# The head of each image woven into the layers of the next one, with its state and residual sum kept in HBM

## Chip, cores and metric

The kernel runs on one core of one Trainium2 chip. The metric is the device time of one launch in microseconds, which covers all eight images of the batch. A launch is repeated and the median is given.

## The reference

The input `x` has shape (8, 8, 256, 256): eight images of eight channels. Layer 0 of the network is a Fourier neural operator on the group-normalised image, added to its input. Layer 1 is a 3x3 dilation of the group-normalised result, again added to its input.

```python
h = _gconv1x1(concat(xg, grid), fc0_w, fc0_b)        # 4 groups, 10 channels each
for i in range(4):
    h1 = _spectral_conv(h, sp_w1[i], sp_w2[i])       # 24 x 12 modes mixed, rest zero
    h2 = _gconv1x1(h, w_w[i], w_b[i])
    h = h1 + h2
    if i < 3:
        h = _gswish(h, betas[i])
h = _gswish(_gconv1x1(h, fc1_w, fc1_b), betas[3])    # 10 -> 128 channels per group
return _gconv1x1(h, fc2_w, fc2_b)                    # 128 -> 2 per group
...
x = x + _L0_conv_ref(_gn(x), ...)
x = x + _L1_conv_ref(_gn(x))                         # max over 3x3 windows, border -2
```

## The kernel before

Images are handled one after another. The state of one image, 40 channels of 256 x 256, lives in SBUF as `h`, 11 chunks of 128 partitions by 4 x 512 numbers. Each of the four layers has the same stages.

- The spectrum of the state is formed. For layer 0 `spectrum_x` takes it from the image by transposes (L204), a Fourier product (L214) and small products (L223, L233). For the later layers each chunk is turned on VectorE as soon as it is written (`turn`, L394) and multiplied with the Fourier table (`transform`, L407: 128 small products of 32 x 32 for a pair of chunks, 256 records in the profile), and `spectrum_h` does the other direction (L268 or L285, then L293).
- `mix` multiplies the modes by the weights, all on VectorE (L322, L326, six of each), and folds them (L338) into `fz`.
- `rows_of` transforms back along one axis (L358 or L363) into the tile `Z`.
- `layer` writes one chunk at a time: 16 products for the pointwise weights (L439 for layer 0, L442 later) and 8 for the other axis (L445) go to two PSUM tiles `p_z`. The document calls these a burst. ScalarE applies Silu from PSUM into `h` (L450). In layer 3 VectorE and ScalarE add a bias instead (L452, L454).

After layer 3, `head` runs 128 steps. In a step, `first` makes 512 hidden values of 128 partitions for each of four groups (L482, two PSUM tiles), ScalarE applies two Silus of 128 x 1024 (L485), and `second` of the step before adds its products (L491) to a sum `acc` that lasts 16 steps. Then `residual` (L496) adds the image on VectorE into the tile `x1`. After step 80 the head is interrupted by `prologue`: the spectrum and the first mix of the next image. After the head, `dilate` takes statistics of `x1`, fetches the neighbour rows by DMA (L522, L523) and works in four pieces (L529 to L542), each sent out by SP (L543).

PSUM is one pool of four tiles of two banks, from which every product takes its tiles:

```python
ps = ctx.enter_context(tc.tile_pool(name="ps", bufs=4, space=PSUM))
def ps_z(name):
    return ps.tile([128, 2, 512], F32, tag="z", name=name)
def ps_a(name):
    return ps_z(name)[:, 0, :]
```

Each engine works through its own queue in order. TensorE's order is the order of the program text within the blocks marked `manual_schedule`. On the other engines a scheduler of the framework chooses the order from its own estimate of when operands are ready. All DMAs are issued by SP.

Of the kernel before, what the change touches and what calls it, by code (L numbers as in the profile page):

```python
# [1 line left out]

# [15 lines left out]
C = 8  # L18
# [18 lines left out]
PIX = 2 * HW  # L37


@with_exitstack  # L40
def fno_dilate_kernel(ctx: ExitStack, tc: tile.TileContext, a: dict, out: bass.AP):
# [6 lines left out]
    ps = ctx.enter_context(tc.tile_pool(name="ps", bufs=4, space=PSUM))  # L48

    def ps_z(name):  # L50
        return ps.tile([128, 2, 512], F32, tag="z", name=name)

    def ps_a(name):
        return ps_z(name)[:, 0, :]
# [10 lines left out]
    def load_x(b):  # L65
        t = sb.tile([128, 4096], F32, tag="x", bufs=1, name=f"x_{b}")
        nc.sync.dma_start(t, a["x"][b].rearrange("c (p f) -> (c p) f", p=16))
        return t

    x_tiles = {0: load_x(0)}  # L70
# [12 lines left out]
    eh_f = load("eh_f", (NQ * CS, 3, NBLK, 32))  # L83
# [16 lines left out]
    for c in range(NCH):  # L100
        nc.gpsimd.memset(h[:, c], 0.0)
    fz = const.tile([128, WID, G, 32], F32, tag="fz", name="fz")
# [66 lines left out]
    def group_stats(chunks, name):  # L169
        n = len(chunks)  # L170
        st = sb.tile([128, n, 6], F32, tag="bn", name=f"bn_{name}")
        for i, c in enumerate(chunks):
            nc.vector.bn_stats(st[:, i, :], c)
        mv = sb.tile([128, 2], F32, tag="mv", name=f"mv_{name}")
# [3 lines left out]
        mr = sb.tile([128, 2], F32, tag="mr", name=f"mr_{name}")  # L178
# [12 lines left out]
    def spectrum_x(b):  # L191

        x = x_tiles[b]
        mr = group_stats([x[:, 512 * i : 512 * (i + 1)] for i in range(8)], f"x{b}")
        a0 = sb.tile([128, 128, 16], F32, tag="A", bufs=1, name=f"a0_{b}")
        for half in range(2):
            xn = x[:, 2048 * half : 2048 * (half + 1)]
            nc.vector.tensor_scalar(xn, xn, mr[:, 0:1], mr[:, 1:2], ALU.subtract, ALU.mult)
            xn = xn.rearrange("p (r w) -> p r w", r=8)
            xt = sb.tile([128, 2, 8, 128], F32, tag="ht", name=f"xt_{b}_{half}")  # L200
            for r in range(0, 8, 2):
                t = ps_a(f"p_xt_{b}_{half}_{r}")
                for i in range(4):
                    nc.tensor.transpose(  # L204
                        t[:, 128 * i : 128 * (i + 1)],
                        xn[:, r + i // 2, 128 * (i % 2) : 128 * (i % 2 + 1)], ident,
                    )
                nc.vector.tensor_copy(
                    xt[:, :, r : r + 2, :], t.rearrange("p (r f c) -> p f r c", r=2, f=2)
                )  # L210
            for i in range(2):
                p = ps_a(f"p_a0_{b}_{half}_{i}")
                for f in range(2):
                    mm(p[:32, :], fw[:, f, :], xt[:, f, 4 * i : 4 * i + 4, :],  # L214
                       start=f == 0, stop=f == 1)
                r0 = 8 * half + 4 * i
                nc.vector.tensor_copy(
                    a0[:32, :, r0 : r0 + 4], p[:32, :].rearrange("p (r c) -> p c r", r=4)
                )
        x2 = sb.tile([128, C, 2, 32], F32, tag="xs", name=f"x2_{b}")  # L220
# [6 lines left out]
        nc.vector.tensor_copy(x2.rearrange("p c f k -> p (c f k)"), t)  # L227
        p = ps_a(f"p_xs_{b}")
# [14 lines left out]
        prod = sb.tile([128, 6, G, WID, 5], F32, tag="ht", name=f"prod_{b}")  # L243
# [8 lines left out]
        return bt, mr  # L252
# [5 lines left out]
    def spectrum_h(b, l, at):  # L258

        rows = sb.tile([128, NBLK * WID * 128], F32, tag="big", bufs=1, name=f"AT_{b}_{l}")  # L260
        if l % 2 == 1:

            view = rows.rearrange("p (i g k) -> p i g k", g=G, k=32)
            for j0 in range(0, NBLK * WID, 8):
                n = min(8, NBLK * WID - j0)
                t = ps_z(f"p_at_{b}_{l}_{j0}")
                for i in range(n):
                    nc.tensor.transpose(  # L268
                        t[: NQ * CS, i // 4, 128 * (i % 4) : 128 * (i % 4 + 1)],
                        at[:, :, :, j0 + i], ident)  # L270
                dst = rows[: NQ * CS, 128 * j0 : 128 * (j0 + n)]
                src = t[: NQ * CS].rearrange("p u w -> p (u w)")[:, : 128 * n]
# [4 lines left out]
            eh, m = eh_f, NQ * CS  # L277
            read = lambda blk, k0: view[:m, WID * blk : WID * (blk + 1), :, k0 : k0 + 3]
        else:

            view = rows.rearrange("p (g i k) -> p i g k", g=G, k=32)
            for i in range(4):
                cut = at[:, NBLK * WID * i : NBLK * WID * (i + 1), :]
                over = bass.AP(cut.tensor, cut.offset, [cut.ap[0], cut.ap[1], [1, 32]])
                nc.vector.transpose(rows[:, 960 * i : 960 * (i + 1)].rearrange("p (i r) -> p i r", r=32), over)  # L285
            eh, m = eh_q, 128
            read = lambda blk, k0: view[:m, WID * blk : WID * (blk + 1), :, k0 : k0 + 3]
        p = ps_a(f"p_b_{b}_{l}")
        for k in range(2):
            for n in range(2 * NBLK):  # L290
                term, blk = n // NBLK, n % NBLK
                for q in range(4):
                    mm(p[part(q), 120 * k : 120 * k + 120], eh[:, spectrum_table(k, term), blk, :],  # L293
                       read(blk, 12 * term + 3 * q), start=n == 0, stop=n == 2 * NBLK - 1)
# [10 lines left out]
        return bt  # L305

    def load_sw(b, l):
        tiles = []
        for k in range(3):
            t = sb.tile([128, G, 2 * WID, WID], F32, tag="xs", name=f"sw_{b}_{l}_{k}")  # L310
            nc.sync.dma_start(t.rearrange("p g m i -> p (g m i)"), a["spw"][l, k])
            tiles.append(t)
        return tiles

    def mix(b, l, bt):

        s = [sb.tile([128, 3, G, 2, WID], F32, tag=f"S{i}", bufs=1, name=f"S{i}_{b}_{l}") for i in range(2)]
        sw = load_sw(b, l)
        for k in range(3):
            for k2 in range(2):  # L320
                pr = sb.tile([128, G, 2 * WID, WID], F32, tag="ht", name=f"pr_{b}_{l}_{k}_{k2}")
                nc.vector.tensor_tensor(  # L322
                    pr, sw[k], bt[:, k2, k].unsqueeze(2).to_broadcast([128, G, 2 * WID, WID]),
                    ALU.mult,
                )
# [6 lines left out]
        nc.vector.tensor_tensor(f[:, 1], s[0][:, :, :, 1, :], s[1][:, :, :, 0, :], ALU.add)  # L332

# [7 lines left out]
        for q in range(4):  # L341
# [4 lines left out]
            else:  # L346
                nc.scalar.copy(dst, src)  # L347

    def rows_of(b, l):

        z = sb.tile([128, CS, NQ, 32], F32, tag="big", bufs=1, name=f"Z_{b}_{l}")
        nc.gpsimd.memset(z[:, :, :, NBLK * WID :], 0.0)
        zv = z[:, :, :, : NBLK * WID].rearrange("p r f (n o) -> p o n r f", n=NBLK)
        for o in range(0, WID, 2):
# [10 lines left out]
            for u in range(2):  # L365
                src = p[:, u, : NBLK * CS * NQ]
                if l % 2 == 0:
                    dst, src = zv[:, o + u].rearrange("p n r f -> p n f r"), src.rearrange("p (n f r) -> p n f r", n=NBLK, r=CS)
# [7 lines left out]
        return z  # L376


    def layer(b, l, z, mr=None):
        at = None  # L380
        if l == 1:

            at = sb.tile([128, G * NBLK * WID + 1, 24], F32, tag="A", bufs=1, name=f"A_{b}_{l}")
            nc.gpsimd.memset(at[:, :, CS:], 0.0)
            nc.gpsimd.memset(at[:, G * NBLK * WID], 0.0)
        elif l < 3:
            at = sb.tile([128, NQ, CS, 32], F32, tag="A", bufs=1, name=f"A_{b}_{l}")
        ht = {}

        def turn(c):  # L390

            if c % 2 == 0:
                ht[0] = sb.tile([128, 2, NQ, 2, 8, 32], F32, tag="ht", name=f"ht_{b}_{l}_{c}")
            nc.vector.transpose(  # L394
                ht[0][:, c % 2].rearrange("p f s v i -> p (f s v i)"),
                h[:, c].rearrange("p f w -> p (f w)"),
            )
            return (ht[0], c // 2, 2) if c % 2 == 1 else ((ht[0], c // 2, 1) if c == NCH - 1 else None)

        def transform(t, d, n):  # L400

            m = 2 * n * NBLK * WID
            pair = [ps_z(f"p_d_{b}_{l}_{d}_{i}") for i in range(2)]
            for v in range(8):
                for f in range(NQ):
                    for q in range(NQ):
                        mm(pair[q // 2][part(f), q % 2, :m], fw8[part(q), v, :],  # L407
                           t[part(q), :n, f, :, v, : NBLK * WID], start=v == 0, stop=v == 7)
            for i in range(2):
                src = pair[i][:, :, :m]  # L410
                if l == 1:
                    dst = at[:, : G * NBLK * WID].rearrange("p (q i) r -> p q i r", q=NQ)[
                        :, 2 * i : 2 * i + 2, :, 4 * d : 4 * d + 2 * n]
                    src = src.rearrange("p q (r i) -> p q i r", i=NBLK * WID)
                else:
                    dst = at[:, 2 * i : 2 * i + 2, 4 * d : 4 * d + 2 * n, : NBLK * WID]
                    src = src.rearrange("p q (r i) -> p q r i", i=NBLK * WID)
                if i == 0:
                    nc.vector.tensor_copy(dst, src)
                else:  # L420
                    nc.scalar.copy(dst, src)  # L421
# [8 lines left out]
        ready = []  # L430
        with tc.manual_schedule(engines={PE}):
            for c in range(NCH):
                pair = [ps_z(f"p_z_{b}_{l}_{c}_{i}") for i in range(2)]
                for f in range(NQ):
                    for q in range(NQ):
                        o = pair[q // 2][part(f), q % 2, :]
                        if l == 0:
# [279 lines left out]
```

## Time and profile before

| | us |
|---|---|
| runs shown: median (lowest to highest of 3) | 5554.56 (5548.94 to 5554.61) |
| the profiled execution | 5550.97 |
| its span, first to last instruction | 5549.1 |
| PE busy in the span | 4317.3 (78%) |
| PE weight loads, beside PE | 1945.8 (35%) |
| DVE busy | 2002.1 (36%) |
| ACT busy | 2848.7 (51%) |
| POOL busy | 38.5 (1%) |
| mean granted TensorE clock | 0.872 |
| HBM read, written | 91.87 MB, 16.78 MB |

Busy times of the engines overlap, so they don't add up to the span. PE is TensorE, DVE is VectorE, ACT is ScalarE, POOL is GpSimd and SP is the engine that issues DMAs. The granted clock is the share of full speed at which TensorE was let run. In lines of the profile, `L482` is a line of the kernel, `out<-in` are tiles, `xN` is the number of instructions, and a bracket at the end of a line of the timeline says how long the engine was idle and what ended it.

### The profile page before, as it was taken

How to read it: one execution, taken by the hardware profiler on the slowest of the kernel's cores; microseconds unless marked ns; L12 is line 12 of the kernel's file. 1: busy time of each engine (PE TensorE's matmuls, PEld its weight loads, DVE VectorE, ACT ScalarE, POOL GpSimd, SP SyncE). 2: the span in 40 equal slices, each digit the busy share in tenths (PEclk: the TensorE clock that was granted, in tenths of full speed). 3: DMA queues.
4: the chain of work that ended last, by engine and by line, in shares of the span. 5: the costliest groups of instructions: out<-in, count | busy, mean ns of one | idle time of the engine just before them, and what ended most of it. 6: DMA issues, size and time to landing. Idle time of an engine off the chain costs nothing.

```text
span 5549.1 us, 169821 instructions
## 1 busy us (share of the span) xinstructions
PE 4317.3 (78%) x80490; PEld 1945.8 (35%) x80490; DVE 2002.1 (36%) x2363; ACT 2848.7 (51%) x3117; POOL 38.5 (1%) x99
## 2 busy tenths in 40 slices
PE   5679876798667986679866798667986679866897
PEld 3442234422344223442234422344223442234421
DVE  6440344403454035530355303453035530355302
ACT  2248642486324863248632486334863248623486
POOL 1000000000000000000000000000000000000000
PEclk8889877999789997899868898689997899978998
DMA  2000000000000000000100000000000000000000
GB/s 75 21 21 9 30 27 21 21 10 29 27 21 22 9 29 27 21 22 9 30 26 21 22 9 29 27 21 22 9 31 26 21 22 12 13 29 18 22 1 17
DMA packets 46814, 121.60 MB, mean 22 GB/s; under 512 B 6783, under 2 KB 26471, under 8 KB 42983
## 3 DMA queue, kind: packets, MB, share of 16 engines
q1 hardware_dynamic: 46119, 110.75, 6.6%
q8 instruction: 630, 10.32, 0.8%
q14 instruction: 65, 0.53, 0.0%
HBM read 91.87 MB, written 16.78 MB: 20 GB/s over the span
## 4 chain that ended last, share of the span: by engine, by line
PE 73%; DVE 16%; issue 8%; ACT 2%; DMA 0%; DVEq 0%; SPq 0%; ACTq 0%
PE p_fc L482 22%; PE p_fc L491 18%; PE p_d L407 10%; PE p_z L445 7%; PE p_z L442 5%; DVE pr L322 3%; PE p_z L439 2%; DVE S L326 2%; PE p_g L363 2%; PE p_b L293 2%; PE p_at L268 1%; PE p_g L358 1%; PE p_f L338 1%; DVE h L429 1%; DVE m L529 1%
## 5 line engine op out<-in xcount | busy, mean ns | idle before, releaser
L485 ACT ACTIVATE act<-p_fc 128x1024 f32<-128x1024 f32 x2048 | 1982.5, 1021 | 249.0 <-PE p_fc L482 233.0
L482 PE MATMUL p_fc<-h,c_w 32*128 32x512 f32 x8192 | 1298.2, 642 | 7.8 <-DVE h L452 4.1
L491 PE MATMUL p_fc<-act,c_w 128*32 128x512 f32 x8192 | 1104.9, 605 | 0.3
L394 DVE STREAM_TRANSPOSE ht<-h 128x2048 f32<-128x2048 f32 x264 | 599.7, 2297 | 601.0 <-ACT h L450 600.3
L407 PE MATMUL p_d<-ht,c_fw 32*32 32x120 f32 (+1 forms) x36864 | 565.0, 283 | 276.3 <-issue 274.1
L482 PEld LDWEIGHTS p_fc<-h,c_w 32*128 32x128 f32 x8192 | 439.6, 184 | 864.8 <-issue 545.9
L450 ACT ACTIVATE h<-p_z 128x1024 f32<-128x1024 f32 x528 | 511.9, 1021 | 382.4 <-PE p_z L445 382.3
L407 PEld LDWEIGHTS p_d<-ht,c_fw 32*32 32x32 f32 x36864 | 467.3, 109 | 391.6 <-issue 346.2
L496 DVE SCALAR_TENSOR_TENSOR x<-p_fc,c_b,x 128x512 f32<-128x512 f32 x64 | 48.1, 752 | 1501.2 <-PE p_fc L491 1215.3
L445 PE MATMUL p_z<-c_binv,Z 32*128 32x256 f32 x5632 | 463.1, 443 | 14.1 <-ACT Z L375 9.0
L347 ACT COPY fz<-p_f 32x240 f32<-32x240 f32 x64 | 35.5, 554 | 819.7 <-DVE fz L345 819.7
L491 PEld LDWEIGHTS p_fc<-act,c_w 128*32 128x32 f32 x8192 | 163.7, 108 | 792.9 <-issue 726.7
L445 PEld LDWEIGHTS p_z<-c_binv,Z 32*128 32x128 f32 x5632 | 287.4, 205 | 363.7 <-issue 350.1
L338 PE MATMUL p_f<-F,c_fold 32*32 32x120 f32 x1024 | 58.3, 402 | 442.1 <-DVE F L331 442.1
L442 PE MATMUL p_z<-h,c_wt 32*32 32x512 f32 x8448 | 352.6, 610 | 20.8 <-issue 20.7
L421 ACT COPY A<-p_d 128x240 f32<-128x240 f32 x144 | 49.8, 346 | 598.8 <-PE p_d L407 598.8
L375 ACT COPY Z<-p_g 128x264 f32<-128x264 f32 x160 | 96.4, 629 | 385.9 <-DVE Z L373 360.5
L358 PE MATMUL p_g<-c_rowg,fz 128*128 128x264 f32 x320 | 116.2, 536 | 226.8 <-ACT Z L375 203.3
L429 DVE TENSOR_SCALAR h<-h,mr_x 128x2048 f32<-128x2048 f32 x88 | 117.4, 1334 | 382.0 <-DMA h<-in_xp 381.5
L338 PEld LDWEIGHTS p_f<-F,c_fold 32*32 32x32 f32 x1024 | 44.9, 163 | 450.7 <-issue 352.1
L322 DVE TENSOR_TENSOR pr<-sw,B 128x800 f32<-128x800 f32 x192 | 182.2, 980 | 0.6
L326 DVE TENSOR_REDUCE S<-pr 128x80 f32<-128x800 f32 x192 | 181.2, 975 | 0.8
(131 smaller groups left out, 2287.5 us busy)
## 6 DMA issues: line engine op xcount, KB each, us to landing
sw<-in_spw SPq DMA_DIRECT2D x96, 400.0 KB
x<-in_x SPq DMA_DIRECT2D x16, 2048.0 KB
h<-in_xp SPq DMA_DIRECT2D x352, 48.0 KB
out<-o SPq DMA_DIRECT2D x32, 512.0 KB
x<-x SPq DMA_DIRECT2D x16, 112.0 KB
c_wt<-in_wt SPq DMA_DIRECT2D x1, 256.0 KB
x<-x SPq DMA_DIRECT2D x16, 15.0 KB
c_w<-in_w SPq DMA_DIRECT2D x1, 192.0 KB
```

The lines of the kernel that those rows point to most:

```text
L322: nc.vector.tensor_tensor(pr, sw[k], bt[:, k2, k].unsqueeze(2).to_broadcast([128, G, 2 * WID, WID]), ALU.mult,)
L326: nc.vector.tensor_reduce(s[k2][:, k].rearrange("p g s o -> p (g s o)"), pr.rearrange("p g m i -> p (g m) i"), AX.X, ALU.add,)
L358: mm(p[:, u, : NBLK * CS * NQ], fz[:, o + u].rearrange("p g k -> p (g k)"), rowg.rearrange("p n j r -> p (n j r)"), start=True, stop=True)
L394: nc.vector.transpose(ht[0][:, c % 2].rearrange("p f s v i -> p (f s v i)"), h[:, c].rearrange("p f w -> p (f w)"),)
L407: mm(pair[q // 2][part(f), q % 2, :m], fw8[part(q), v, :], t[part(q), :n, f, :, v, : NBLK * WID], start=v == 0, stop=v == 7)
L429: nc.vector.tensor_scalar(hc, hc, mr[:, 0:1], mr[:, 1:2], ALU.subtract, ALU.mult)
L442: mm(o, wt[part(q), l, g, :], h[part(q), c, f, :], start=True, stop=False)
L445: mm(pair[q // 2][:, q % 2, HW * s : HW * (s + 1)], z[part(q), 2 * c + s].rearrange("p f o -> p (f o)"), binv[part(q), :], start=False, st ...
L450: nc.scalar.activation(dst, pair[i], AF.Silu)
L482: mm(pair[g // 2][:, g % 2, :], w1[gs, blk, :], h[gs, c, j, :], start=True, stop=True)
L485: nc.scalar.activation(act[:, 2 * i : 2 * i + 2, :], pair[i], AF.Silu)
L491: mm(acc[32 * g : 32 * g + 32, :], w2[:, g, 15 - rb : 47 - rb], act[:, g, :], start=rb == 0, stop=rb == 15)
```

## The change

The head of image b no longer follows its layers. After layer 3 each chunk of the state is stored to HBM (`stored`), and the next image's layers start at once. `layers` is now a generator that gives way after each small part and says how many units the part counts. The main loop runs head steps of the image before so that 128 of them spread evenly over one image's units. `unit` emits a burst and then the second half of whatever came before it, which was held back in `late`. The head reads the state back from HBM, a chunk at a time. The residual sum goes to HBM too (`y_rows`), and the dilation, now in eight pieces of two output rows (`DR = 2`), reads four rows per piece into the single tile `yin`. A dilation advances by one of its three parts with each head step of the following image. Image 0's layers and the last head and dilation have no partner.

PSUM becomes three tiles of two banks (`z`) and two tiles of one bank (`a`). The tiles for images, turned chunks and products share one constant tile `turned`. The transform's result goes back into `Z`. The loads of the head and all DMAs of the dilation are issued by POOL; the stores of the state are issued by SP.

```diff
-    ps = ctx.enter_context(tc.tile_pool(name="ps", bufs=4, space=PSUM))
+    ps = ctx.enter_context(tc.tile_pool(name="ps", bufs=2, space=PSUM))
+    dram = ctx.enter_context(tc.tile_pool(name="dram", bufs=2, space=bass.MemoryType.DRAM))
     def ps_z(name):
-        return ps.tile([128, 2, 512], F32, tag="z", name=name)
+        return ps.tile([128, 2, 512], F32, tag="z", bufs=3, name=name)
     def ps_a(name):
-        return ps_z(name)[:, 0, :]
+        return ps.tile([128, 512], F32, tag="a", bufs=2, name=name)
...
+    turned = const.tile([128, 3, 2048], F32, tag="turned", name="turned")
+    yin = const.tile([128, DR + 2, HW + 2], F32, tag="yin", name="yin")
...
+    def unit(burst, after):
+        burst()
+        if late[0] is not None:
+            late[0]()
+        late[0] = after
...
     # layer()
+        for c in range(NCH):
+            before = ready[c - 1] if l < 3 and c > 0 else None
+            unit(partial(burst, c), partial(transform, before) if before is not None else None)
+            yield 1
+        if l < 3:
+            yield 2
+            if before not in done:
+                flush()
+            transform(ready[NCH - 1])
+            yield 1
     # burst(c), at its end
+            if l < 3:
+                ready.append(turn(c))
+            else:
+                nc.sync.dma_start(stored[c], h[:, c].rearrange("p f w -> p (f w)"))
...
+    def load_state(b, c, stored):
+        t = sb.tile([128, NQ, PIX], F32, tag="hs", name=f"hs_{b}_{c}")
+        nc.gpsimd.dma_start(t.rearrange("p f w -> p (f w)"), stored[c])
     # head(), second(n) at the end of 16 steps
+                y = box["y"]
+                nc.vector.scalar_tensor_tensor(y, acc, b2, y, ALU.add, ALU.add)
+                nc.vector.bn_stats(stats[:, t, :], y)
+                whole = y_rows[b % 2][:]
+                nc.gpsimd.dma_start(
+                    bass.AP(whole.tensor, whole.offset + (1 + 2 * t) * HW, [[16 * HW, 128], [1, 512]]), y)
+        for n in range(STEPS):
+            if n % 12 == 0 and n // 12 + 1 < NCH:
+                hs[n // 12 + 1] = load_state(b, n // 12 + 1, stored)
+            unit(partial(first, n), partial(second, n))
+            yield
...
     # dilate()
+        for r in range(0, 16, DR):
+            nc.gpsimd.dma_start(
+                yin[:, :, 1 : HW + 1],
+                bass.AP(whole.tensor, whole.offset + r * HW, [[16 * HW, 128], [HW, DR + 2], [1, HW]]))
+            yield
...
+            nc.vector.tensor_tensor(m, yin[:, :, 0:HW], yin[:, :, 1 : HW + 1], ALU.max)
...
+            yield
...
+            nc.vector.tensor_tensor(o, o, yin[:, 1 : DR + 1, 1 : HW + 1], ALU.add)
+            nc.gpsimd.dma_start(o_rows[:, HW * r : HW * (r + DR)], o.rearrange("p r w -> p (r w)"))
+            yield
...
+    with tc.manual_schedule(engines={PE}):
+        for b in range(n_img):
...
+            for n in layers(b, stored):
+                count += n
+                if total is not None:
+                    share += n * STEPS / total
+                    while share >= 1.0:
+                        share -= 1.0
+                        step()
```

The function `step` advances the oldest head by one step and, beside it, the oldest dilation by one part.

## The prediction

> **What bounds the kernel now.** I read the slices of the span first, then groups, waits and, for one image, the timeline.
>
> ```profile
> PE   5679876798667986679866798667986679866897
> DVE  6440344403454035530355303453035530355302
> ACT  2248642486324863248632486334863248623486
> PEclk8889877999789997899868898689997899978998
> ```
>
> Eight images, eight waves: ACT climbs to 8 where a head runs and falls to 2 where layers run; DVE does the opposite. PE is full in heads only. Nothing is full throughout, so the time is a sum of stages, each with its own limit. Stretches of one image (core time, PE busy, PEld, DVE, ACT, POOL, granted clock, DMA):
>
> ```profile
> 740.00:760.00 20.00, 0.00 (x0) 0.00 (x0) 20.00 (x27) 0.00 (x0) 0.00 (x0) 0.50 0.13 52
> 980.00:1020.00 40.00, 31.70 (x1399) 20.73 (x1385) 19.03 (x12) 15.28 (x19) 0.00 (x0) 1.00 0.02 4
> 1100.00:1120.00 20.00, 20.00 (x152) 5.38 (x144) 0.00 (x0) 17.89 (x19) 0.00 (x0) 1.00 0.05 11
> ```
>
> The first is the dilation: PE idle, clock at half. The second is inside a layer, the third the head: PE full, ACT at 89%. The timeline of a layer's two-chunk cycle:
>
> ```profile
> 1008.02 1.15 PE L445 MATMUL p_z<-c_binv,Z 32*128 32x256 f32 x16
> 1009.09 1.18 PE L442 MATMUL p_z<-h,c_wt 32*32 32x512 f32 x32
> 1009.20 1.94 ACT L450 ACTIVATE h<-p_z 128x1024 f32<-128x1024 f32 x2 [3.86 <-PE p_z L445]
> 1010.21 1.15 PE L445 MATMUL p_z<-c_binv,Z 32*128 32x256 f32 x16
> 1011.28 2.56 PE L407 MATMUL p_d<-ht,c_fw 32*32 32x120 f32 x180
> 1015.86 1.17 PE L407 MATMUL p_d<-ht,c_fw 32*32 32x120 f32 x72 [2.02 <-issue]
> ```
>
> A burst (L442 then L445) takes 2.18 us, its two Silus on ACT 1.94; a transform (L407, 256 records at about 14 ns) takes 3.6 us plus a hole in which nothing was issued. Two waits matter (total us, times, longest):
>
> ```profile
> PE p_f L338 <- DVE F L331: 442.1, 32, 20.3
> PE p_d L407 <- issue: 274.1, 183, 2.5
> ```
>
> The first is the mix on DVE: 11.3 us (848.6 to 859.9) with PE empty. The second is the hole.
>
> Image 1, 724 to 1418 us, splits so: dilation and first rows to the first burst 43 us; layers 0, 1, 2 from first burst to the following table work 72.5, 67.5, 61 (sum 201); the three pieces between layers 32, 31, 33.5 (sum 96.5); layer 3 24; the head 175 + 111 = 286, for 128 steps of 2.18 (L482 1.15, L491 1.0); the prologue inside it 43. Sum 694.
>
> **What the Trainium skill says.** "TensorE: Matmul & The Clock Gate", Part 1 (HAM clock gate): after an idle window of about 3.4 us the array clock halves. The trace agrees: 0.50 at 740 to 760. "Runtime: NRT & Kernel Launch", Instruction fetch mechanics: instructions come in blocks of 256. The trace fits two blocks of lead: the holes come after 130 to 240 transform records, each of these being a load and a multiply. The page gives PE room for 2048, which the trace does not support. "DMA: Bandwidth & Descriptors", Anatomy of one DMA (SWDGE): a POOL-issued DMA costs 2.0 us + bytes/436e3; no run shows one yet. "TensorE: Matmul & The Clock Gate", Engine queue depths: ACT and DVE are strict FIFO; so I use the instruction order of the built program.
>
> **The change part by part, per woven image.**
>
> *Removed:* the x1 tile with its four halo copies on SP (L522, L523), the prologue inside the head, the dilation with PE idle. *Added:* 11 stores and 11 loads of the state, 8 stores of y, 8 loads of yin of four rows each, 8 `out` stores of 256 KB for 4 of 512 KB. *Moved:* the head's steps into the next image's layers, the dilation into the one after, one piece in three steps.
>
> *Floor.* At full clock PE work is 128 steps 279, 44 bursts 96, 18 transforms 63 (15 pairs of 3.6, three singles of 2.9), p_g 22 and transposes, tables and spectrum 36, both scaled from their rows: 496 us. What comes on top is waiting, and it is the question here.
>
> *Layers 0 to 2.* PE order per two chunks: burst, second, first, transform, burst, second, first. PSUM falls from four z buffers to three, taken in turn. A step adds two Silus in ACT's FIFO behind the burst's two. From a burst's end, ACT needs 0.17 + 3 x 1.0 to free the third buffer, PE has second and first (2.15) to do: the transform's second buffer is 1.3 us late, and the next burst without a transform between 1.15 late. The burst after a transform waits for its copies (two of 0.28 and the way there): 0.85. The hole stays, about 1.7, as a transform still is 512 instructions in a row. Cycle: 4.36 + 4.36 + 3.6 + 1.7 + 1.3 + 1.15 + 0.85 = 17.3. Five cycles 86.5, one burst 2.2, 1.6 extra steps 3.4, tail (3.4 steps 7.5, last transform 4.6) 12: 104 us with 16 steps inside. Less 34.9 for those: 69, against 67 before. Three layers: lose 6. The two-chunk cycle before, about 10.6, plus two steps is 15: here weaving gives nothing.
>
> *Layer 3.* Same third-buffer wait: 5.15 per chunk and an extra step in seven, 60 us with 12.6 steps; net 32.5 against 24: lose 8.5.
>
> *Between layers.* The mix's 11.3 + 1.3 us on DVE are covered by 7 steps (15.2). p_at 4.4, p_b 3.4, 13.7 steps 29.9, p_f with the four alternating fz copies 3.7, p_g about 4: 45 us; for layer 2, where DVE turns the table, 42; for layer 3 again 45, sum 132. p_g's copies stand on ACT behind a step's two Silus, which I count as covered by the next step; net 132 - 89.6 = 42.5 against 96.5: gain 54.
>
> *Image start (spectrum, mix, rows, dilation of an earlier image).* DVE order matters here: six of eight dilation pieces lie among the spectrum's copies, and a piece's first max stands right behind the last add of the piece before, on one yin buffer. DVE work: eight pieces of 5.46 (two max of 1024 at 1.22 as in L532; of 512, estimated from the same rows, three at 0.75 and a scaling 0.45; two edges 0.32) 44, eleven L429-like scalings at 1.33 15, mix 12, statistics, copies and products 20: 91. Waits for yin: each load is out store, then load on POOL's queue, behind DVE's add: 1.0 (my estimate of the issue) + 2.0 + 524288/436e3 = 4.3, fully exposed in about four pieces, 17 in all; the first (y store, then load) 8. Sum 116; behind it p_g and six steps 18: 134 us. PE's own work there is about 80, so it stands about 50: 8 at p_sv, whose operand is queued on DVE behind the first yin load, 8 in the first half of the spectrum and 12 in the second, 8 at p_xs and p_f, 14 at p_g, whose fz copies stand behind the last piece. Steps cannot fill this, since PE's queue is in order and the waiting instruction stands ahead of them. Net of 26 steps (56.7) 77, against 43 + 43 before: gain 9. Cost of a load, both ends: 2.7 (small SP copies that DVE awaited at L525, issue to use) to 10.
>
> *State through HBM.* 88 stores of 1 MB on SP in layer 3, 88 loads on POOL two ahead: a load's estimate 4.4 us against 26 us for 12 steps even undisturbed. Hidden; I take 0, at worst 2 us per load where it slows PE's instruction blocks: 20 per image. It cannot gain. The xp loads on SP now stand between these stores, but their scalings are due only in the next image start: 0, or up to 10 if a store lags. On POOL an hs load waits for its buffer with y loads, y stores and Z's memsets queued behind; by the instruction order none of these is due before that buffer falls free, so 0; in the worst case a memset delays p_g by one step interval, about 5. The Sqrt of the two statistics still switches ACT's table (1.28 each way): same number, 0.
>
> Woven image: 134 + 3 x 104 + 60 + 132 = 638, against 694.
>
> *Ends.* Image 0, not woven: heads started at 398; three buffers cost 2.1 per cycle (16.5 of them) and 1.2 per chunk in layer 3, constants are now loaded ahead of x (8): 454. Last head 279. Last dilation alone: 8 + 8 x (4.3 + 5.5) = 86 and 2 for the store, against 38.
>
> Sum: 454 + 7 x 638 + 279 + 88 = 5287, +2 outside the span: 5290. The profiled execution took 5551 (span 5549.1) and the median is 5554.6, so they compare directly: -4.7%.
>
> **Rivals.** (a) PE packs nearly full: the waits overlap the holes, or DVE drains faster, so an image falls to 500 to 580 us; 454 + 7 x 540 + 367 = 4600, at best 4300. For it: the floor of 497. Against: two Silus of burst and step share one FIFO. (b) Slower: DVE stands for yin at each image start. If a load takes 10 us instead of 4.3, seven pieces cost 40 us more per image, 280 in all: 5570; from about 9.6 us per load on it decides (262 us of gain over seven images and seven pieces is 5.3). For it: one yin buffer, write and read through HBM, POOL issuing in order behind waits. Against: 512 KB is small and the rings are nearly idle (2 to 5%). (c) The added waits in layers return the whole gain (2.3 us more per cycle than I count, times 16.5 is 38 per image, 266): 5556, no change. For it: sixteen holes and PSUM waits per image whose overlap I only reckoned by hand.
>
> **How the numbers follow.** Mild gain (5000 to 5530) 0.64; (a) below 5000 0.10; within 0.2%, about what a measurement of this kernel can tell from no change, 0.04 (mostly from c); slower 0.22, (b) and the upper part of (c). So faster 0.74. Likeliest 5290. The range 4980 to 5630 leaves about 0.1 out on each side: it takes in 45 us per image down and 48 up.
>
> **What would show it.** PE about 80% busy at clock near 1.0 in all woven slices, ACT near 5 to 6 tenths without waves. Waits of fc1 and transform on ACT near 1.2 us each; holes at the transform still about 1.7; DVE waiting on yin some 4 us per piece. If woven images take under 580 us, the buffer argument is wrong; if over 690, the yin or the hole is mis-sized. Instruction holes gone would refute the fetch reading.

## The result, and the profile after

The changed kernel takes 5608.6 us (median of four runs, 5602.1 to 5624.8), the kernel before 5554.6 us beside it: ratio 1.0102, 95% interval 1.0078 to 1.0127. It is 1.0% slower, where 5290 us was forecast. A ratio, here and below, is the time over that of the kernel before, measured beside the same run. The profiled execution has a span of 5622.9 us, 74 more than before. These are its busy shares in tenths, for comparison with the four rows shown for the kernel before:

```profile
PE   5667899968998788887989779997799977999892
DVE  5334333362333633245333442334433353332303
ACT  1223555545555445554555445554455544555682
...
PEclk7779899979999799998999888998899988999996
```

The waves of ACT are gone: it stands at 5 tenths from the second image on, as forecast. PE is busier (7 to 9 tenths in the woven images, least at their starts). So the weaving took place. Two spans of the timeline are unwoven, the first 3 to 4 slices and the last 3, and both are longer than before. What DVE waits for tells of a new cost (us in total, times, longest):

```profile
DVE m L575 <- DMA yin<-y_rows: 203.8, 48, 7.0
DVE yin L571 <- DMA yin<-y_rows: 76.1, 8, 11.8
DVE yin L573 <- DMA yin<-y_rows: 43.6, 8, 6.4
```

That is 323 us of waiting for the dilation's input. Stretches of one woven image: the image start (last burst of layer 3 to the first of layer 0), layer 0, layer 1 (columns: us, then PE, PEld, DVE, ACT, POOL busy, granted clock, DMA share, GB/s):

```profile
1801.00:1958.00 157.00, 102.36 (x632) 33.15 (x628) 89.42 (x136) 64.88 (x73) 18.12 (x25) 0.75 0.29 87
1958.00:2076.00 118.00, 103.59 (x2324) 42.71 (x2320) 29.51 (x24) 55.78 (x67) 1.62 (x3) 0.89 0.05 16
2119.80:2225.30 105.50, 91.44 (x2310) 40.79 (x2308) 29.51 (x24) 53.72 (x65) 1.62 (x3) 1.00 0.05 18
```

At the image start PE idles for 55 of 157 us and has a clock of 0.75. Layer 0, which has the same instructions as layer 1 but for one product, runs at 0.89. The next table holds the stages that all runs below are read by, worked out from the timeline: means over images 2 to 6 in us (image 0 is the first), then the three ends. An image start runs from the last burst of layer 3 to the first of layer 0. "Image 0" runs to the statistics of image 1's x, "last head" from the statistics of one y to the next, "last dilation" from there to the end of the span. Kernels are named after their runs; in e12 the head stands in the image start.

| kernel | span | start | layer 0 | 1 | 2 | three gaps | layer 3 | image | image 0 | last head | last dilation |
|---|---|---|---|---|---|---|---|---|---|---|---|
| predicted | 5287 | 134 | 104 | 104 | 104 | 132 | 60 | 638 | 454 | 279 | 88 |
| after | 5623 | 157 | 119 | 105 | 108 | 134 | 58 | 681 | 515 | 307 | 97 |
| e1 | 5509 | 109 | 121 | 106 | 117 | 150 | 60 | 664 | 517 | 294 | 97 |
| e2 | 5348 | 121 | 120 | 106 | 107 | 134 | 58 | 646 | 524 | 286 | 41 |
| e3 | 5554 | 157 | 112 | 104 | 109 | 134 | 58 | 674 | 507 | 306 | 96 |
| e4 | 5611 | 155 | 121 | 105 | 109 | 134 | 58 | 682 | 520 | 305 | 96 |
| e5 | 5419 | 129 | 119 | 106 | 109 | 134 | 58 | 655 | 522 | 292 | 57 |
| e6 | 5576 | 157 | 120 | 106 | 107 | 135 | 58 | 682 | 467 | 306 | 97 |
| e7 | 5602 | 156 | 115 | 106 | 110 | 136 | 58 | 680 | 520 | 292 | 96 |
| e8 | 5284 | 128 | 112 | 106 | 107 | 136 | 58 | 646 | 458 | 292 | 57 |
| e9 | 5573 | 157 | 116 | 105 | 109 | 135 | 58 | 680 | 482 | 307 | 97 |
| e10 | 5298 | 109 | 119 | 106 | 109 | 146 | 58 | 647 | 460 | 294 | 57 |
| e11 | 5457 | 58 | 146 | 126 | 119 | 157 | 64 | 670 | 449 | 295 | 57 |
| e12 | 5774 | 350 | 74 | 77 | 75 | 102 | 38 | 715 | | 286 | 57 |

Layer 0 varies by some 3 us between runs that do not touch it.

### The profile page after: what moved, and what is told of

It reads as the page before. It is cut to its first block, busy times and chain, and to the rows that moved or that the text cites. A ratio compares the mean times of both kernels' runs of the same rounds, so it can differ in the third digit from the quotient of the medians.

```text
span 5622.9 us, 171099 instructions
## 1 busy us (share of the span) xinstructions
PE 4647.9 (83%) x80490; PEld 1907.3 (34%) x80490; DVE 2109.8 (38%) x2627; ACT 2860.7 (51%) x3269; POOL 280.2 (5%) x428
## 5 line engine op out<-in xcount | busy, mean ns | idle before, releaser
L526 PE MATMUL p_fc<-hs,c_w 32*128 32x512 f32 x8192 | 1458.8, 676 | 62.3 <-DVE o L584 29.1
L421 DVE STREAM_TRANSPOSE turned<-h 128x2048 f32<-128x2048 f32 x264 | 610.2, 2311 | 1082.2 <-ACT h L470 1082.2
L440 PE MATMUL p_d<-turned,c_fw 32*32 32x120 f32 (+1 forms) x36864 | 582.9, 275 | 346.5 <-issue 215.4
L526 PEld LDWEIGHTS p_fc<-hs,c_w 32*128 32x128 f32 x8192 | 485.0, 193 | 860.2 <-issue 360.4
L440 PEld LDWEIGHTS p_d<-turned,c_fw 32*32 32x32 f32 x36864 | 463.9, 106 | 539.8 <-issue 275.2
L461 PE MATMUL p_z<-h,c_wt 32*32 32x512 f32 x8448 | 517.3, 607 | 17.0 <-issue 9.4
L472 DVE TENSOR_SCALAR h<-p_z,c_bias 128x1024 f32<-128x1024 f32 x88 | 112.9, 1283 | 359.5 <-PE p_z L464 359.5
L458 PE MATMUL p_z<-h,wc 6*32 6x512 f32 x2816 | 193.2, 668 | 8.2 <-issue 4.5
L356 DVE TENSOR_TENSOR turned<-sw,B 128x800 f32<-128x800 f32 x192 | 180.5, 980 | 0.8 <-DMA sw<-in_spw 0.6
L358 DVE TENSOR_REDUCE S<-turned 128x80 f32<-128x800 f32 x192 | 179.4, 974 | 0.0
```

The costliest lines, as they stand in the source:

```text
L356: nc.vector.tensor_tensor(pr, sw, bt[:, k2, k].unsqueeze(2).to_broadcast([128, G, 2 * WID, WID]), ALU.mult)
L358: nc.vector.tensor_reduce(s[k2][:, k].rearrange("p g s o -> p (g s o)"), pr.rearrange("p g m i -> p (g m) i"), AX.X, ALU.add,)
L421: nc.vector.transpose(turned[:, c % 3], h[:, c].rearrange("p f w -> p (f w)"))
L440: mm(pair[q // 2][part(f), q % 2, :m], fw8[part(q), v, :], t[part(q), :, f, :, v, : NBLK * WID], start=v == 0, stop=v == 7)
L458: mm(o, wc[k, :], h[k, c, f, :], start=True, stop=False)
L461: mm(o, wt[part(q), l, g, :], h[part(q), c, f, :], start=True, stop=False)
```

## The experiments

**The dilation's wait for yin.** One piece in the image start, on DVE and on POOL:

```profile
1863.99 0.69 DVE L589 TENSOR_TENSOR o<-o,yin 128x512 f32<-128x512 f32 x1
1870.17 1.22 DVE L575 TENSOR_TENSOR m<-yin 128x1024 f32<-128x1024 f32 x1 [5.49 <-DMA yin<-y_rows]
...
1872.57 0.68 DVE L242 COPY turned<-p_xt 128x512 f32<-128x512 f32 x1
...
1864.98 0.55 POOL L590 DMA_DIRECT2D out<-o  x1 [10.65 <-DVE o L589]
1865.51 0.76 POOL L565 DMA_DIRECT2D yin<-y_rows  x1
```

The add of one piece frees yin; POOL issues the store and then the load; the next piece's first maximum stands at the head of DVE's queue for 5.49 us. L242, which the spectrum's next product needs, stands behind it, and so PE waits too. Over the whole run PE's longest waits for other engines are such ones, mostly at the image starts, for what DVE does late, or ACT behind it:

```profile
PE p_g L393 <- ACT fz L380: 98.5, 16, 15.0
PE p_sv_x L192 <- DVE mv_x L190: 79.5, 8, 14.3
PE p_xt L236 <- ACT turned L243: 78.3, 13, 10.7
```

Run e1 moves the pieces away from there, to every second head step inside the layers, and puts POOL in program order:

```diff
+        room[0] = True          # in layer(), around the loop over bursts
...
-        if tails and next(tails[0], 0) == 0:
+        parts[0] += room[0]
+        if tails and room[0] and parts[0] % 2 == 0 and next(tails[0], 0) == 0:
             tails.pop(0)
...
-    with tc.manual_schedule(engines={PE}):
+    with tc.manual_schedule(engines={PE, POOL}):
```

> The dilation's pieces are issued at every second head step inside a layer, and POOL's instructions (with the yin loads) keep program order, so that no piece can be drawn forward into the image start. Theory (dilation and its yin loads stand on DVE ahead of the spectrum's copies, PE waits and loses its clock): from the last burst of layer 3 to the first burst of layer 0, 156 us now, falls to about 108, as in image 1, which has no dilation; layers grow by under 5 each where a piece delays a turn; woven image 682 to about 640, so 5340 us (5300 to 5420). Rival (DVE's work is only moved and delays the turns and transforms by as much): layers grow by about 15 each, 5560 to 5620. Rival (the head steps at the image start are slow by themselves): start stays above 140.

Measured: 5508.1 us, ratio 0.9883 (0.9856 to 0.9910). The start fell to 109 us as the theory said, but the gaps between layers grew by 16 and layer 2 by 9, so a woven image kept 17 of the 48 us. The theory and its first rival were each half right. The timeline of a gap shows why:

```profile
2043.65 1.23 DVE L579 TENSOR_TENSOR m<-yin 128x1024 f32<-128x1024 f32 x1 [7.71 <-DMA yin<-y_rows]
...
2046.78 0.55 DVE L380 COPY fz<-p_f 32x240 f32<-32x240 f32 x1
...
2049.15 1.11 PE L400 MATMUL p_g<-c_rowg,fz 128*32 128x66 f32 x32 [8.51 <-ACT fz L382]
```

The scheduler, which still orders DVE, put one piece ahead of the fz copy. It waited 7.71 us for yin, and p_g came 8.5 us late. The wait had moved with the piece. The start of e1 also has a wait of its own: in POOL's program order the load of the next head's first state stands behind the last store of y, and fc1 waited 7.5 to 10.2 us for it in every start of images 2 to 7. In the changed kernel it did not wait there. Run e2 takes the load away and leaves DVE's work where it was:

```diff
-            nc.gpsimd.dma_start(
-                yin[:, :, 1 : HW + 1], ...)
             yield
```

> The loads of yin are left out, so the dilation works on a constant tile; its work on DVE stays where it was. Theory A (the waits for yin, some 41 us per image in the trace, are what the dilation costs at the image start): start 156 to about 120, six images x 38 and some 40 from the last dilation: about 5340 us. Theory B (DVE's own 44 us of dilation is what costs, waits overlap with PE's steps): start stays near 145 to 150, about 5520 us with the last dilation shorter by 40.

Measured: 5350.8 us, ratio 0.9599 (0.9570 to 0.9628); start 121 us, last head 286, last dilation 41. Theory A holds: without the waits the start is 36 us shorter. The other 12 us down to e1's 109 go with DVE's own work on the dilation; that may cost more, since e1's start contains the wait for the state. Image 1 of the changed kernel, which has no dilation and no earlier head to finish, takes 84 us, not the 108 that the expectation of e1 gives it. Run e5 asks whether a second buffer does the same with nothing left out. It also reorders the maximum, which shortens DVE's work:

```diff
+    yins = [const.tile([128, DR + 2, HW + 2], F32, tag=f"yin{i}", ...) for i in range(2)]
...
+        fetch(0)
         for r in range(0, 16, DR):
+            if r + DR < 16:
+                fetch(r + DR)
+            yin = yins[r // DR % 2]
...
-            m = sb.tile([128, DR + 2, HW], F32, tag="m", bufs=1, ...)
-            nc.vector.tensor_tensor(m, yin[:, :, 0:HW], yin[:, :, 1 : HW + 1], ALU.max)
+            m = sb.tile([128, DR, HW + 2], F32, tag="m", bufs=1, ...)
+            nc.vector.tensor_tensor(m, yin[:, 0:DR], yin[:, 1 : DR + 1], ALU.max)
```

> Two yin buffers, each piece's load issued one piece ahead; to make room the maximum is taken over rows first, then over columns (m is then half as large and two of its four passes are half as long, about 1.1 us less per piece), and y has one buffer. Nothing is left out. Theory (the waits for yin cost 36 us at each image start, and more at the ends): image start 157 to about 118 us, woven image to about 643, last head near 286, last dilation from 91 to about 45: about 5340 us (5300 to 5390). Rival (the loads are slow because they run beside PE's, and a buffer only moves the wait): start stays above 140, over 5480 us.

Measured: 5415.4 us, ratio 0.9699 (0.9678 to 0.9720). The time misses the range of the theory, and the start is 129, not 118: more than a third of the waits are left, most of them at an image's first piece, whose load follows the last store of y:

```profile
DVE yin L578 <- DMA yin<-y_rows: 68.4, 8, 11.2
DVE m L582 <- DMA yin<-y_rows: 35.6, 19, 3.9
DVE yin L580 <- DMA yin<-y_rows: 15.5, 7, 3.0
```

That is 119 us against 323. In one start (1786 to 1914 us of e5) the waits are 18.7 us against 41.4, and DVE is busy for 79.5 us against 89.4, so some 10 of the 28 us gained come with less work on DVE and not with the buffer.

**Layer 0.** Run e3 gives its pointwise product the shape of the other layers:

```diff
-                        k = slice(32 * q, 32 * q + 6)
-                        mm(o, wc[k, :], h[k, c, f, :], start=True, stop=False)
+                        mm(o, wc[part(q), :], h[part(q), c, f, :], start=True, stop=False)
```

> Layer 0's pointwise product uses all 32 rows of each quarter instead of 6 (the added rows of the weight are zero), so a burst has the shape of the other layers' ones. Theory (products of 6 rows let the granted clock fall: 0.67 to 0.95 in layer 0 against 1.00 in layers 1 and 2): layer 0 from 118 to about 106 us in woven images, clock near 1.0 there, eight images x 12: about 5515 us. Rival (the clock falls because of the image start or of the holes at the transform, not of the shape): layer 0 stays at 118, 5600 to 5620 us.

Measured: 5563.5 us, ratio 0.9989 (0.9977 to 1.0000); layer 0 from 119 to 112 us. The same stretch of image 3 as above:

```profile
1934.00:2045.00 111.00, 96.32 (x2320) 41.48 (x2288) 29.52 (x24) 55.03 (x66) 1.62 (x3) 0.96 0.05 17
```

The clock is 0.96 instead of 0.89. The shape matters, for about half of what layer 0 has over layer 1. The rival, that a slow image start leaves a low clock behind, does not fit: in image 1 of the changed kernel the start has a clock of 0.98, and layer 0 after it takes 119 us at 0.88 all the same; in every image of e3 the first 15 us of layer 0 have 1.00. What the rest is (112 against 104) stays open.

**PSUM and ACT in the layers.** A cycle of two chunks takes 16.8 us (2160.5 to 2177.2), close to the 17.3 of the prediction. Its waits (matmuls of one cycle of the changed kernel):

```profile
2167.19 1.14 PE L461 MATMUL p_z<-h,c_wt 32*32 32x512 f32 x28 [0.19 <-ACT act L529]
...
2170.33 1.31 PE L526 MATMUL p_fc<-hs,c_w 32*128 32x512 f32 x8
...
2172.64 2.31 PE L440 MATMUL p_d<-turned,c_fw 32*32 32x120 f32 x166 [0.68 <-ACT act L529]
2176.26 1.25 PE L440 MATMUL p_d<-turned,c_fw 32*32 32x120 f32 x79 [1.31 <-issue]
```

To test that ACT's queue is behind them, e4 leaves out the second Silu of each head step and e9 the second of each burst:

```diff
-            for i in range(2):
-                nc.scalar.activation(act[:, 2 * i : 2 * i + 2, :], pair[i], AF.Silu)
+            nc.scalar.activation(act[:, 0:2, :], pair[0], AF.Silu)
...
+                    if i == 0:
                         nc.scalar.activation(dst, pair[i], AF.Silu)
```

> The second Silu of each head step is left out (fc2 reads the first one's half twice), so a step gives ACT 1.0 us of work instead of 2.0 and its second PSUM pair falls free at once; PE's instructions are the same. Theory (three PSUM pairs behind one ACT queue hold PE in the layers): the two-chunk cycle 16.8 to about 15.2 us, three layers and layer 3 shorter by some 30 us per woven image, seven images: about 5400 us. Rival (the instruction holes and the clock set the cycle): it stays at 16.5 or more and the time above 5560 us. The last head, where PE is full, doesn't change.

> The second Silu of each burst in layers 0 to 2 is left out (half of the state keeps its old values), so a burst's second PSUM pair falls free at once and the Silus of the head step start 1.0 us earlier; PE's instructions are the same. The run that left out the step's second Silu could not test the PSUM waits, since PE waits for the third of the four Silus and only the fourth was taken away. Theory (three pairs behind ACT's queue set the two-chunk cycle above PE's own 12.3 us): cycle 16.8 to about 15.3 us, woven image 681 to about 655, and image 0 some 15 shorter: about 5410 us. Rival (holes and clock set the cycle): 16.5 or more, above 5560 us.

Measured: 5611.5 us (ratio 1.0070, 1.0043 to 1.0097) and 5582.9 us (1.0031, 1.0020 to 1.0043). No layer of a woven image got shorter in either; what e9 gained is in image 0, where the turns start earlier. Both theories fell; e4 could not have shown more, since the Silu that it leaves out is the one behind the Silu that PE waits for. The same place of the cycle in e9:

```profile
2104.50 1.14 PE L527 MATMUL p_fc<-hs,c_w 32*128 32x512 f32 x8
...
2106.81 2.30 PE L440 MATMUL p_d<-turned,c_fw 32*32 32x120 f32 x167 [0.85 <-ACT act L530]
2110.53 1.25 PE L440 MATMUL p_d<-turned,c_fw 32*32 32x120 f32 x78 [1.41 <-issue]
```

With three Silus in the queue instead of four the transform still waits for the step's first Silu. From the start of fc1 (L526, L527 in e9) to the transform's products after the wait it is 2.31 us in both kernels: the way through fc1's products, its own 1.0 us Silu and back to the pair. So ACT's queue is not what holds PE here. Whether a fourth pair would take the wait away was not tried.

**Image 0.** Without head steps between, a pair's transform stands behind the turn that takes over one of its three slots (it reads the later chunk there, too):

```profile
250.71 1.94 ACT L470 ACTIVATE h<-p_z 128x1024 f32<-128x1024 f32 x2 [1.39 <-PE p_z L464]
252.68 2.31 DVE L421 STREAM_TRANSPOSE turned<-h 128x2048 f32<-128x2048 f32 x1 [1.01 <-ACT h L470]
...
255.05 1.34 PE L440 MATMUL p_d<-turned,c_fw 32*32 32x120 f32 x57 [4.37 <-DVE turned L421]
```

A burst's Silus and its turn are thus on PE's path, 4.37 us per cycle. Run e6:

```diff
             unit(partial(burst, c), ...)
+            if b == 0:
+                flush()
```

> In image 0, which has no head steps between its bursts, a pair's transform is issued right after the next burst instead of one burst later, where it waits for the turn that has taken over one of its three slots (4.4 us of waiting on DVE in the trace). Theory (this wait is what image 0 lost beyond the prediction): its layers 102, 90, 90 to about 80, 70, 70, first statistics of image 1 at about 455 instead of 515: about 5555 us. Rival (three PSUM pairs and the low clock cost it): no more than 15 us gained.

Measured: 5586.2 us, ratio 1.0017 (1.0003 to 1.0031); image 0 467 instead of 515 us, its layers 86, 76, 73. That is most of the 60 us of the theory and far more than the 15 of its rival. The transform now waits 1.05:

```profile
253.09 3.16 PE L440 MATMUL p_d<-turned,c_fw 32*32 32x120 f32 x235 [1.05 <-DVE turned L421]
```

**The state through HBM.** Run e7:

```diff
-                hs[n // 12 + 1] = load_state(b, n // 12 + 1, stored)
+                hs[n // 12 + 1] = load_state(b, 1, stored) if n == 0 else hs[n // 12 - 1]
```

> Of the eleven loads of the state per image only two are kept, and the head works on these two again and again; the stores stay. The prediction's step (the state's way through HBM is hidden): woven images stay at 681, last head from 307 to about 296 because its one late load is gone, 5590 to 5610 us. Rival (the loads, issued on POOL behind waiting stores, hold the head or slow PE's instruction blocks): woven image shorter by 10 to 20, about 5500 us.

Measured: 5595.5 us, ratio 1.0038 (1.0027 to 1.0049); woven image 680 against 681, last head 292. The nine loads that are gone cost at most a few us in a woven image, and about 15 us once. Where, the last head of the changed kernel shows (the stores of the state, and the first two loads, were not tested):

```profile
5297.96 0.74 DVE L546 SCALAR_TENSOR_TENSOR y<-p_fc,c_b,y 128x512 f32<-128x512 f32 x1
5298.76 1.93 PE L542 MATMUL p_fc<-act,c_w 128*32 128x512 f32 x8 [4.58 <-DVE y L546]
...
5310.35 0.55 POOL L590 DMA_DIRECT2D out<-o  x1 [4.94 <-DVE o L589]
5310.89 0.53 POOL L513 DMA_DIRECT2D hs<-stored  x1
...
5317.69 1.24 PE L526 MATMUL p_fc<-hs,c_w 32*128 32x512 f32 x4 [11.68 <-DMA hs<-stored]
```

The addition of y stands on DVE behind a piece of dilation; the load of the next state stands on POOL behind that dilation's out store, and fc1 waits 11.68 us for it.

**The mends together, and what weaving is worth.** e8 is e5, e6 and e3 in one kernel, with no edit beyond theirs; e10 adds the placing of e1, at bursts 0 to 7 of layers 0 to 2; e11 also issues no head step before an image's first burst; e12 is e8 with each head run alone after its layers, and with the transform order of e6 in every image:

```diff
+            room[0] = l < 3 and c in (0, 1, 2, 3, 4, 5, 6, 7)   # e10, e11
...
             for n in layers(b, stored):
+                if not began[0]:                                # e11
+                    continue
...
-                if total is not None:
+                if False:                                       # e12
```

> Two yin buffers as in the run of that name, the new order in image 0, and 32 rows in layer 0's pointwise product together. If the three causes are separate, the gains add: about 270 + 55 + 55 less than 5609, so 5230 us (5190 to 5290), faster than the kernel before by 5 to 6%. If they share a wait, it stays above 5300.

> The version with all three mends (two yin buffers, image 0's order, 32 rows), and the dilation's parts only at the bursts 0 to 7 of layers 0 to 2, with POOL in program order. Theory (what the dilation still costs at the image start, 128 against 108 us without it, goes away, and layers have room on DVE): start near 109, layers and gaps together no more than 10 longer, woven image 646 to about 637, 5230 us. Rival (as in the first run with the dilation in layers, the pieces slip into the gaps between layers and take the gain back): 5280 to 5330 us.

> As the run with spread parts, and no head step is issued before the first burst of an image: the 128 steps are spread over the rest (1.45 per unit). Theory (at the image start the clock is at half, so the 23 to 27 steps there cost up to 4.3 us each and hardly fill anything): start falls from 109 to about 70, the rest grows by about 25 steps x 2.2 = 55: woven image within 20 of the spread run, 5220 to 5380 us. Rival (steps at the start are hidden in DVE's chain): start stays above 90, woven image 30 to 50 longer, 5450 to 5600 us.

> The version with all three mends, but not woven: each image's head runs alone after its layers, the dilation of the image before beside it. It gives what weaving itself is worth with three PSUM pairs. From image 0's stages (start 50 and the statistics, layers 73, 77, 75, gaps 103, layer 3 38) and the head alone (284): about 640 to 700 per image, 5300 to 5650 us. If weaving is worth what its packing suggests (646 per woven image), this run is slower than the woven one by 200 to 350 us; if it is no slower, the gain of the mended version comes from the mends alone.

Measured: e8 5285.8 us, ratio 0.9469 (0.9452 to 0.9486), faster than both kernels and inside the range expected; against the changed kernel the three mends are worth 0.060 of the time before when added up from their own runs, and 0.063 together. e10 5297.6 us, ratio 0.9513 (0.9497 to 0.9529): again the start fell (to 109), and the gap after layer 0 (44 to 55) and layer 0 itself (112 to 119) gave it back. The time is the rival's. But e10 has the wait for the state that e1 has, 58.3 us in seven waits against 4.6 in one in e8; without it the spread pieces might have gained as the theory said, which was not tried. e11 5459.3 us, ratio 0.9807 (0.9791 to 0.9824): start 58, lower than the 70 of the theory, but the rest grew by 74 instead of 55, so that the time is the rival's while its reason (a start above 90) is not. Why it grew by more stays open. e12 5776.4 us, ratio 1.0375 (1.0356 to 1.0394), 490 us slower than e8, more than expected. Busy shares of e8 and e12:

```profile
PE   4668889978899788888989888988889988999995
...
ACT  2225555555556455565555555555555545555784
```

```profile
PE   5679966799667995679966799667996679876895
...
ACT  2228822388223872238722387223872248632485
```

The waves of e12 are those of the kernel before, yet e12 is some 210 us slower than that kernel. This is the price of the rest of the change: its layers 0 to 2 take 226 us against 201 before, its layer 3 38 against 24. Three PSUM pairs instead of four would do this, but the cause was not separated.

From e12 to e8, what a head step adds in each stage: in the gaps (136 - 102) / 41 = 0.8 us, in layers 0 to 2 (325 - 226) / 48 = 2.1, in layer 3 20 / 12.6 = 1.6, against 2.2 alone (285 / 128). At the image start it is (109 - 58) / 26 = 2.0, from e10 to e11, of which about 0.3 is e10's wait for the state; in image 1, without that wait, it is (83 - 51) / 25 = 1.3. So the gaps hide most: there weaving gains (2.2 - 0.8) x 41, near 57 us, of the 70 us per image between e12 and e8. Layers 0 to 2 hide next to nothing.

## Why the prediction was wrong, step by step

In the profiled executions the sum missed by 336 us. Split at the statistics of each y, it is image 0 +61, image 1 -23, six images with dilation +260, last head +28, last dilation +9 (rounded). Of the 43 us that a woven image took too long, 23 are the image start and 15 layer 0.

- **Image start, 134 us: failed, 157.** DVE's work was right (91 predicted, 89.4 in the window). The waits for yin were not: 17 + 8 = 25 us predicted, 41.4 measured in that window (24.3 + 11.8 + 5.3). This is the step that failed most. The first wrong term is "fully exposed in about four pieces": all eight loads were waited for. The second is the load itself: 4.3 us from the add were predicted, 5.5 to 7 were measured where nothing lay between. The other third of the 23 us lies behind DVE's chain (about 26 us where 18 was predicted). On PE's side the stands were forecast at about the right places (13.4 us at p_sv_x, 13.2 at p_xt and 14.1 at p_g in that window; 55 in all against some 50), but between them its own work took 102 us instead of about 80, at a clock of 0.75. e2 shows what all the waits for yin carry: 36 us of the stage. Rival (b) had this mechanism, but not its size: its threshold of 9.6 us per load was never reached. Less was enough, because other terms took part of the gain.
- **The price of a load.** The Trainium skill, "DMA: Bandwidth & Descriptors", Anatomy of one DMA, gave an estimate of 3.2 us for 512 KB without the issue; the trace has 4.8 from issue to landing. For 1 MB, 4.4 against 5.1. The measurement decides; for 512 KB it is half as much again.
- **Layers at 104 us: right for layers 1 and 2 (105, 108), failed for layer 0 (119).** Layer 0 was priced at full clock like the others, although the prediction's own split has it longest before the change (72.5 against 67.5 and 61). It had 0.89, and e3 shows 7 of the 15 us to come from products of 6 rows. The cycle, 17.3 against 16.8, was right in its sum. Its working, ACT's queue ahead of the third pair, was not: e9 took a Silu out from ahead of it and the cycle stayed.
- **Between layers 132 (134), layer 3 60 (58): right.** "Here weaving gives nothing" for the layers and the gain in the gaps are borne out by e8 against e12.
- **State through HBM 0: right** for the nine loads that e7 leaves out; the stores were not tested. In the last head the step missed that a load of state can stand behind a dilation on POOL.
- **Ends.** Image 0 was costed by PSUM alone (2.1 us per cycle), and the turn stands nowhere in its sum; 4.37 us per cycle of it was on PE's path, and e6 gives back 48 of the 61 us. The last head was counted at 2.18 per step with nothing beside it; e2 returns 21 of its 28 us, so the dilation's loads in it are the main cause; the late load of the state (e7, 15 us) hangs on the same chain.

The signs to watch for were mixed: no ACT waves and PE at 83% came as forecast; the holes at the transform stayed (215 us in 136 of them, 1.6 each where 1.7 was forecast), the waits of the transform on ACT were 0.7 instead of 1.2, and DVE waited 5.5 to 7 us on yin instead of 4 where nothing hid it. A woven image of 681 us stayed just under the 690 that was to mean a mis-sized yin or hole; it was mis-sized all the same. Rivals (a) and (c) did not occur: the image was far from 580 us, and the cycle was no longer than counted.

Why the whole is slower than before: seven woven images take 615 + 4088 = 4703 us, about 125 less than seven of the pitch before ((5549 - 398 - 286 - 38) / 7 = 690 us), and the two ends lost about 200 (image 0 +117, last dilation +59, last head +21). With the mends, e8 has both: 646 us per image and shorter ends. That it lands at 5286, beside the 5290 of the forecast, does not bear the forecast out: it is another kernel, with two buffers for yin and less work on DVE.

## What to carry to other kernels

Weaving pays only where the host stage leaves the engine empty: price it stage by stage as "cost of one more step here", not as idle time over the span. Work that is cut in pieces to fill gaps brings its loads along, and with one buffer each piece shows its whole load at the head of an in-order queue; look at who stands behind it. Work that is moved can also make others wait: the order that took the dilation out of the image start put a load of state behind a store there. The first and the last pass of a woven loop have no cover, so they are to be priced apart.

## What was not expected of the hardware

- Products over 6 of 32 rows lowered the granted clock: 0.89 with them, 0.96 with 32 rows, at the same number of instructions (e3). The Trainium skill, "TensorE: Matmul & The Clock Gate", Part 1 (HAM clock gate), speaks of how busy PE is; in this kernel PE's busy share there was about the same (104 of 118 us, 96 of 111).
- The hole in the transform's instructions did not shrink with the wait ahead of it: in e9 a wait of 0.85 and a hole of 1.41, in the changed kernel 0.68 and 1.31, with the same cycle of about 16.8 in both. What sets the place of the holes is the number of instructions: in the traces of the changed kernel and of the kernel before, every distance between two transform holes of over 0.9 us (121 and 148 of them), counted in instructions of PE (products, weight loads and semaphore instructions), is a multiple of 256 to within one. This fits the prediction's reading of instruction blocks.
